# PSUM as two single banks and two groups of three, with the order of head steps around it

## The chip, the cores and the metric

The kernel runs on one core of a Trainium2 chip. The metric is the device time of one execution in microseconds (us). A few per mille separate its runs. Engines are named as in the profile: PE is the matrix engine (TensorE), DVE the vector engine, ACT the scalar engine with activations, POOL is GpSimd, SP the engine that issues most transfers. Each runs its own instructions strictly in the order in which the kernel wrote them, and waits for other engines on semaphores. Matmuls write to PSUM, eight banks of 512 float32 values on each of 128 partitions; ACT and DVE read it from there.

## The reference

Eight images of 8 channels and 256 x 256 pixels go through two layers, all in float32. `_gn` is a group normalization (4 groups of channels).

```python
def _L0_conv_ref(x, ...):           # x: normalized image, G=4 groups, WID=10, 12 x 12 modes
    h = _gconv1x1(concat(x, gridx, gridy), fc0_w, fc0_b)
    for i in range(4):
        h1 = _spectral_conv(h, sp_w1[i], sp_w2[i])   # rfft2, 12 x 12 modes mixed, irfft2
        h2 = _gconv1x1(h, w_w[i], w_b[i])
        h = h1 + h2
        if i < 3:
            h = _gswish(h, betas[i])
    h = _gswish(_gconv1x1(h, fc1_w, fc1_b), betas[3])    # 10 -> 128 channels a group
    return _gconv1x1(h, fc2_w, fc2_b)                    # 128 -> 2 channels a group

x = x + _L0_conv_ref(_gn(x), ...)
x = x + _L1_conv_ref(_gn(x))         # dilation: the maximum of each 3 x 3 window
return x
```

The part around the loop is called the *head* below: fc1, swish, fc2, the sum with x and the statistics of the result. The second layer is the *dilation*.

## The kernel before, in words

**State.** The hidden state of one image lies in `h`, 11 chunks c (`NCH`) of 128 partitions x 4 x 512 values. Three lines of the image share a partition group of 30 rows (`NBLK` x `WID`), so there are 4 partition groups of 32.

**PSUM.** One helper gives out all of it: `ps_z` (L56), four buffers of two banks each, in rotation. `ps_a` (L59) takes such a buffer and uses its first bank. An operation over four groups q takes a pair of buffers: groups 0 and 1 in the first, 2 and 3 in the second. Whoever wants a buffer waits until the buffer's last user but three has been read.

**A layer** (layers 0 to 2 of an image, `layer`, L448) goes over the chunks:

- `burst(c)` (L494): 16 + 8 products into a pair of buffers p_z (the 1x1 convolution, L504 or L501, and the way back from the spectrum, L507), then two ACT operations of 1024 values that write h[c] (swish, L513).
- `turn(c)` (L451): two DVE transpositions of h[c] into `turned`, a ring of three chunks.
- `transform(k)` (L462): the column transform of chunks 2k and 2k+1, 32 products into a pair p_d, copied back into `turned` by DVE (first buffer) and ACT (second), L476.
- `gather(k)` (L478): p_u, 4 products that sum partitions, copied by DVE into the spectrum's input `zt`.

After the last chunk `spectrum_h` (L342) turns `zt` four times on DVE and makes the row transform p_b (L357) on PE; `mix` (L377) does the spectral weights on DVE, 12 operations of 800 values, and folds the result with p_f (L403); `rows_of` (L422) expands the rows, p_g, two of ten channels at a time, ten copies into `zt`.

**Layer 3** only has bursts (without swish, L515, and a store of the chunk to DRAM, `stored`). Between them stands the start of the *next* image, `start` (L560): its statistics and spectrum (`spectrum_x`, L246) and its first mixing. It is a generator called `side` in `layer`, and each `next(side)` records one piece of it: for instance four BN statistics on DVE; or their aggregate on DVE, p_st on PE and what DVE makes of it.

**The head** of the image before is cut into 128 steps (`head`, L631). `first(n)` (L645) reads a stored chunk from DRAM, makes fc1 for the four groups (p_fc1, L651, four products of 512 columns, two passes each) into a pair of buffers, and two ACT operations of 1024 values (swish, L653) into `act`. `second(n)` (L656) makes fc2 of two steps into one bank (L673), which DVE adds to y (L676, L678); every 16 steps y is finished, gets its statistics (L684) and goes to DRAM. In the loop (L691) step n first does `second(n - 4)` when n is even, then `first(n)`.

**The dilation** of the image before that (`dilate`, L702) is a generator, too: per two rows of each partition one load (POOL's queue), about eight DVE operations in several pieces, and a store.

**Who sets the order.** No scheduler: PE, DVE and ACT get their instructions as `fno_dilate_kernel` records them. The main loop (L768) runs over the yields of the layers, and decides at each whether to record a head step: a tuple such as `(1,)` is that many steps, each with one piece of the dilation (`tail`) after it; a number is a share of a step, times `scale`, added up until a whole step is due; "odd" or "even" records one more step if the number of the next one hasn't that parity. In image 0 there is no head to record (`scale` is None), and its layers stand alone. After image 7 the whole last head, 128 steps, stands alone. The head of an image gets all its 128 steps during the next image.

So a round of a layer (L539) is: burst, gather, step (fc2, fc1), dilation piece, turn, burst, transform, step (fc1), dilation piece, turn. A chunk of layer 3 (L532) is: burst, piece of the next image, step (fc1), dilation piece, piece of the next image, step (fc2, fc1), dilation piece.

Of the kernel before, what the change touches and what calls it, by code (L numbers as in the profile page):

```python
# [10 lines left out]
F32 = mybir.dt.float32  # L11
# [8 lines left out]
HW = 256  # L20
NPIX = HW * HW
G = 4
WID = 10
# [21 lines left out]
def fno_dilate_kernel(ctx: ExitStack, tc: tile.TileContext, a: dict, out: bass.AP):  # L45
# [9 lines left out]

    def ps_z(name):  # L56
        return ps.tile([128, 2, 512], F32, tag="z", bufs=4, name=name)

    def ps_a(name):  # L59
        return ps_z(name)[:, 0, :]  # L60

    def part(i):
        return slice(32 * i, 32 * i + 32)
# [89 lines left out]
    wc = const.tile([128, 32], F32, tag="wc", name="wc")  # L153
    p = ps_z("p_wc")
    for g in range(G):
# [37 lines left out]
    def copy(i, dst, src):  # L193
        if alone[0] and i % 2:
            nc.scalar.activation(dst, src, AF.Identity)  # L195
        else:
            nc.vector.tensor_copy(dst, src)  # L197

    def copy_2(i, dst, src):
        if i % 2:  # L200
            nc.scalar.activation(dst, src, AF.Identity)  # L201
        else:
            nc.vector.tensor_copy(dst, src)  # L203


# [40 lines left out]
    def spectrum_x(b, out_):  # L246
# [55 lines left out]
        a3 = a3.rearrange("p (j k) -> p j k", j=2)  # L302
        pair = [ps_z(f"p_xs_{b}_{i}") for i in range(2)]
        for k in range(2):
            for term in range(2):
                for q in range(4):
                    for g in range(G):
                        mm(pair[g // 2][part(q), g % 2, 6 * k : 6 * k + 6], unf[part(g), spectrum_table(k, term), :],
                           a3[part(g), :, 12 * term + 3 * q : 12 * term + 3 * q + 3],
                           start=term == 0, stop=term == 1)  # L310
        xe4 = xe.rearrange("p (s k) g j -> p s g j k", s=2)
        for k in range(2):
            for i in range(2):
                nc.vector.tensor_copy(
                    xe4[:, k, 2 * i : 2 * i + 2, 0:2, :],
                    pair[i][:, :, 6 * k : 6 * k + 6].rearrange("p g (j k) -> p g j k", j=2),
                )
        yield 1.4
# [13 lines left out]
    def spectrum_table(k, term):  # L332

        return 0 if k == term else (1 if k == 0 else 2)
# [87 lines left out]
    def rows_of(b, l):  # L422

        zv = zt[:, :, :, : NBLK * WID].rearrange("p r f (n o) -> p o n r f", n=NBLK)
        for o in range(0, WID, 2):
            p = ps_z(f"p_g_{b}_{l}_{o}")
            for u in range(2):
                if l % 2 == 0:
                    mm(p[:, u, : NBLK * CS * NQ], fz[:, o + u].rearrange("p g k -> p (g k)"),
                       rowg.rearrange("p n j r -> p (n j r)"), start=True, stop=True)  # L430
                else:
                    for g in range(G):
                        for j in range(NQ):
                            mm(p[part(j), u, NBLK * CS * g : NBLK * CS * (g + 1)], fz[:, o + u, g, :],  # L434
                               rowg[:, :, j, :], start=True, stop=True)
            for u in range(2):
                src = p[:, u, : NBLK * CS * NQ]
                if l % 2 == 0:
                    dst = zv[:, o + u].rearrange("p n r f -> p n f r")
                    src = src.rearrange("p (n f r) -> p n f r", n=NBLK, r=CS)  # L440
                else:
                    dst = zv[:, o + u].rearrange("p n r f -> p f n r")
                    src = src.rearrange("p (f n r) -> p f n r", f=NQ, n=NBLK)
                copy(u, dst, src)
            yield 0.7


    def layer(b, l, out_, stored, side):  # L448
        group_in_f = l % 2 == 1

        def turn(c):  # L451

            dst = turned[:, c % 3].rearrange("p (s f x) -> p f s x", s=2, f=NQ)
            for i in range(2):
                nc.vector.transpose(  # L455
                    dst[:, 2 * i : 2 * i + 2], h[:, c, 2 * i : 2 * i + 2].rearrange("p f (s x) -> p f s x", s=2))
# [5 lines left out]
        def transform(k):  # L462


            cs = chunks_of(k)
            n, lo = len(cs), cs[0] % 3
            step = cs[-1] % 3 - lo if n == 2 else 1
            t = turned[:, lo : lo + step * (n - 1) + 1 : step].rearrange("p n (r v i) -> p n r v i", r=2 * NQ, v=8)
            pair = [ps_z(f"p_d_{b}_{l}_{k}_{i}") for i in range(2)]
            for v in range(8):  # L470
                for q in range(NQ):
                    mm(pair[q // 2][part(v % 4), q % 2, : 240 * n], fw8[part(q), v, :],  # L472
                       t[part(q), :, :, v, : NBLK * WID], start=v < 4, stop=v >= 4)
            e = turned[:, (2 * k + 1) % 3, : 960 * n].rearrange("p (q x) -> p q x", q=NQ)
            for i in range(2):
                copy_2(i, e[:, 2 * i : 2 * i + 2], pair[i][:, :, : 240 * n])  # L476

# [16 lines left out]
        def burst(c):  # L494
            pair = [ps_z(f"p_z_{b}_{l}_{c}_{i}") for i in range(2)]
            for f in range(NQ):
                for q in range(NQ):
                    o = pair[q // 2][part(f), q % 2, :]
                    if l == 0:
                        k = slice(32 * q, 32 * q + 6)  # L500
                        mm(o, wcn[k, :], h[k, c, f, :], start=True, stop=False)  # L501
                    else:
                        g = f if group_in_f else q
                        mm(o, wt[part(q), l, g, :], h[part(q), c, f, :], start=True, stop=False)  # L504
            for s in range(2):
                for q in range(NQ):
                    mm(pair[q // 2][:, q % 2, HW * s : HW * (s + 1)],  # L507
                       zt[part(q), 2 * c + s].rearrange("p f o -> p (f o)"), binv[part(q), :],
                       start=False, stop=s == 1)
            for i in range(2):  # L510
                dst = h[:, c, 2 * i : 2 * i + 2, :]
                if l < 3:
                    nc.scalar.activation(dst, pair[i], AF.Silu)  # L513
                else:
                    nc.scalar.activation(dst, pair[i], AF.Identity, bias=bias3)  # L515
            if l == 3:
                nc.sync.dma_start(stored[c], h[:, c].rearrange("p f w -> p (f w)"))
# [11 lines left out]
        if l == 3:  # L529

            yield "odd"
            for c in range(NCH):  # L532
                burst(c)
                for _ in range(LAST):
                    next(side, None)
                    yield (1,)
            return
        yield "even"
        for k in range((NCH + 1) // 2):  # L539
            c = 2 * k  # L540
            burst(c)
            if k > 1:
                gather(k - 2)
            yield (1,)
            turn(c)
            if c + 1 < NCH:
                burst(c + 1)
            if k > 0:
                transform(k - 1)
            yield (1,)  # L550
            if c + 1 < NCH:
                turn(c + 1)
        out_["sw"] = [load_sw(l + 1, 0), load_sw(l + 1, 1)]
# [77 lines left out]
    def head(b, stored, stats):  # L631
# [13 lines left out]
        def first(n):  # L645

            k, blk = n // 32 * NCH + n % 32 // NBLK, n % 32 % NBLK
            act = sb.tile([128, G, 512], F32, tag="act", bufs=4, name=f"act_{b}_{n}")
            pair = [ps_z(f"p_fc1_{b}_{n}_{i}") for i in range(2)]
            for g in range(G):  # L650
                mm(pair[g // 2][:, g % 2, :], w1[part(g), blk, :], hs[k][part(g), :], start=True, stop=True)  # L651
            for i in range(2):
                nc.scalar.activation(act[:, 2 * i : 2 * i + 2, :], pair[i], AF.Silu)  # L653
            acts[n] = act
# [36 lines left out]
        for n in range(STEPS):  # L691
            if n % 32 % NBLK == 0:
                load_state(n // 32 * NCH + n % 32 // NBLK + 2)
            if n % 2 == 0 and n > 3:
                second(n - 4)
            first(n)
            yield
        second(STEPS - 4)
        second(STEPS - 2)
# [61 lines left out]
    with tc.manual_schedule(engines={PE, DVE, ACT}):  # L761
# [3 lines left out]
        for b in range(n_img):  # L765
            stored = [dram.tile([128, NQ * PIX], F32, tag=f"hs{c}", name=f"stored_{b}_{c}") for c in range(NCH)]
            exact, loose, ahead = 0, 0, {}
            for n in layers(b, stored, d, start(b + 1, ahead)):  # L768
                if isinstance(n, str):
                    if count[0] % 2 != (n == "odd") and step():  # L770
                        share -= 1.0
                elif isinstance(n, tuple):
                    exact += sum(n)
                    for _ in range(sum(n)):
                        if scale and step():
                            tail()
                else:
                    loose += n
                    share += n * scale if scale else 0
                    while share >= 1.0:  # L780
                        share -= 1.0
                        step()
# [176 lines left out]
```

## Time and profile before

| | us |
|---|---|
| median of 3 runs | 3963.68 |
| lowest, highest run | 3955.75, 3963.84 |
| the profiled execution | 3959.03 |
| its span, first to last instruction | 3957.2 |
| matmul busy, DVE busy, ACT busy | 3714.1, 2516.6, 2803.0 |
| mean granted PE clock | 0.978 |
| image 0, layers 0, 1, 2 (no head steps) | 52.5, 52.9, 52.8 |
| image 2, layer 0, from first burst to p_b | 88.0 |
| image 2, layer 0 to 1: from p_b to p_f, and to the next burst | 20.4, 19.5 |
| image 2, layer 1, from first burst to p_b | 83.9 |
| image 2, layer 3, up to the first burst of image 3 | 97.2 |
| last head alone, with the last dilation | 282.3 |

The stages are cut at the start of their first PE instruction. One image takes some 470 us, and the first 370 us (loading, image 0) are slower per piece of work. A busy engine in this profile isn't one that computes all the time: an instruction's time holds what it waits for inside the engine, and matmul ends are modelled. Starts are better than busy times: the distance from the start of one group of matmuls to the start of the next (its pitch) can be compared with the same pair elsewhere.

In the lines below, a row in order of time reads: start, duration, engine, source line, operation, tile written <- tiles read, shape, count; in brackets how long the engine had been idle and what released it. A row of a group ends with busy time, mean duration in ns, idle time before and its releasers. A row of a stretch has its time, then the busy time of PE, weight loads, DVE, ACT and POOL with instruction counts, then the granted PE clock (1.00 is full), the share of DMA and GB/s.

### The profile page before, as it was taken

Reading aid. Unit: us, or ns where it says so; the run is one execution under the profiler, and the core shown is the slowest. Engines: PE = TensorE matmul, PEld = TensorE weight load, DVE = VectorE, ACT = ScalarE, POOL = GpSimd, SP = SyncE. Lnnn points to the kernel's source line nnn. Section 1 sums busy time; section 2 is a strip of 40 time slices with the busy share of each in tenths; the row PEclk is TensorE's granted clock in tenths of the full one; section 3 lists DMA queues with packets and bytes.
Section 4 is the critical chain, followed back from the end, with each engine's and each line's share of the span. In section 5 each row is a group of like instructions: output and inputs, shape, how many; then the busy total and the mean of one; then the engine's idle time right before and its main releaser. Section 6 shows DMA issues by size and latency. Waiting matters only on the chain. (4 is left out here: it accounts for less than half of the span.)

```text
span 3957.2 us, 119367 instructions
## 1 busy us (share of the span) xinstructions
PE 3714.1 (94%) x53882; PEld 1423.3 (36%) x53882; DVE 2516.6 (64%) x3740; ACT 2803.0 (71%) x2933; POOL 117.4 (3%) x202
## 2 busy tenths in 40 slices
PE   5667999999999999999999999999999999999996
PEld 2334333333333333333333333333333333333221
DVE  6775656556766666766766576766676666673533
ACT  3335777777777777776777777777777777778886
POOL 1000000000000000000000000000000000000000
PEclk8878999999999999999999999999999999999998
DMA  3014111432225222251223511244221532215311
GB/s 87 14 44 165 55 35 45 145 115 66 61 62 180 87 60 62 86 195 50 60 59 100 195 52 50 62 135 146 60 61 50 175 107 60 60 53 198 103 46 45
DMA packets 114132, 345.08 MB, mean 87 GB/s; under 512 B 16040, under 2 KB 18536, under 8 KB 98200
## 3 DMA queue, kind: packets, MB, share of 16 engines
q1 hardware_dynamic: 95432, 276.32, 22.4%
q0 software_dynamic: 18192, 61.13, 4.7%
q8 instruction: 424, 6.95, 0.7%
q14 instruction: 84, 0.69, 0.1%
HBM read 213.39 MB, written 123.74 MB: 85 GB/s over the span
## 5 line engine op out<-in xcount | busy, mean ns | idle before, releaser
L653 ACT ACTIVATE act<-p_fc 128x1024 f32<-128x1024 f32 x2048 | 1961.1, 1026 | 718.9 <-PE p_fc L651 718.0
L651 PE MATMUL p_fc<-hs,c_w 32*128 32x512 f32 x8192 | 1191.2, 631 | 2.4 <-DVE h L676 1.1
L673 PE MATMUL p_fc<-act,c_w 128*32 128x512 f32 x8192 | 986.7, 600 | 49.8 <-ACT act L653 37.0
L651 PEld LDWEIGHTS p_fc<-hs,c_w 32*128 32x128 f32 x8192 | 389.6, 183 | 683.2 <-ACT act L653 294.9
L455 DVE STREAM_TRANSPOSE turned<-h 128x1024 f32<-128x1024 f32 x528 | 622.6, 1218 | 13.4 <-ACT h L513 13.3
L513 ACT ACTIVATE h<-p_z 128x1024 f32<-128x1024 f32 x528 | 511.9, 1021 | 122.4 <-PE p_z L507 121.8
L678 DVE TENSOR_TENSOR y<-p_fc,y 128x512 f32<-128x512 f32 x392 | 270.6, 690 | 462.4 <-PE p_fc L673 462.4
L673 PEld LDWEIGHTS p_fc<-act,c_w 128*32 128x32 f32 x8192 | 226.5, 109 | 673.0 <-issue 413.3
L507 PE MATMUL p_z<-c_binv,zt 32*128 32x256 f32 x5632 | 409.3, 404 | 1.0 <-ACT zt L195 1.0
L507 PEld LDWEIGHTS p_z<-c_binv,zt 32*128 32x128 f32 x5632 | 258.5, 186 | 307.0 <-issue 288.6
L504 PE MATMUL p_z<-h,c_wt 32*32 32x512 f32 x8448 | 358.5, 603 | 5.6 <-DVE y L678 2.7
L472 PE MATMUL p_d<-turned,c_fw 32*32 32x480 f32 (+1 forms) x9216 | 304.9, 541 | 1.4 <-DVE turned L455 1.4
L197 DVE COPY zt<-p_g 128x264 f32<-128x264 f32 x300 | 161.0, 628 | 178.4 <-PE p_g L434 91.8
L203 DVE COPY turned<-p_d 128x960 f32<-128x960 f32 x144 | 154.3, 1072 | 159.4 <-PE p_d L472 158.9
L515 ACT ACTIVATE h<-p_z,c_bias 128x1024 f32<-128x1024 f32 x176 | 186.6, 1111 | 57.9 <-PE p_z L507 57.6
L387 DVE TENSOR_REDUCE S<-turned 128x80 f32<-128x800 f32 x192 | 188.9, 984 | 5.2
L384 DVE TENSOR_TENSOR turned<-t,B 128x800 f32<-128x800 f32 x192 | 188.5, 982 | 0.2
L348 DVE STREAM_TRANSPOSE turned<-zt 128x960 f32<-128x960 f32 x96 | 175.0, 1849 | 0.8
L201 ACT ACTIVATE turned<-p_d 128x960 f32<-128x960 f32 x144 | 130.3, 905 | 59.4 <-PE p_d L472 59.4
L472 PEld LDWEIGHTS p_d<-turned,c_fw 32*32 32x32 f32 x9216 | 121.3, 103 | 141.3 <-issue 79.0
L504 PEld LDWEIGHTS p_z<-h,c_wt 32*32 32x32 f32 x8448 | 84.8, 103 | 226.4 <-issue 60.3
L486 PE MATMUL p_u<-turned,c_stack 128*32 128x480 f32 (+1 forms) x1152 | 136.2, 544 | 15.6 <-DVE turned L203 15.6
(177 smaller groups left out, 1846.9 us busy)
## 6 DMA issues: line engine op xcount, KB each, us to landing
stored<-h SPq DMA_DIRECT2D x88, 1024.0 KB
hs<-stored SPq DMA_DIRECT2D x352, 256.0 KB
t<-in_spw SPq DMA_DIRECT2D x96, 400.0 KB
yin<-y_rows POOLq DMA_DIRECT2D x56, 512.0 KB, 4.8
h<-in_xp SPq DMA_DIRECT2D x352, 48.0 KB
turned<-in_xw SPq DMA_DIRECT2D x16, 1024.0 KB
y<-in_x SPq DMA_DIRECT2D x56, 256.0 KB
y_rows<-y POOLq DMA_DIRECT2D x56, 256.0 KB, 2.6
```

The costliest lines, as they stand in the source:

```text
L384: nc.vector.tensor_tensor(pr, sw[k], bt[:, k2, k].unsqueeze(2).to_broadcast([128, G, 2 * WID, WID]), ALU.mult)
L387: nc.vector.tensor_reduce(s[k2][:, k].rearrange("p g s o -> p (g s o)"), pr.rearrange("p g m i -> p (g m) i"), AX.X, ALU.add,)
L455: nc.vector.transpose(dst[:, 2 * i : 2 * i + 2], h[:, c, 2 * i : 2 * i + 2].rearrange("p f (s x) -> p f s x", s=2))
L472: mm(pair[q // 2][part(v % 4), q % 2, : 240 * n], fw8[part(q), v, :], t[part(q), :, :, v, : NBLK * WID], start=v < 4, stop=v >= 4)
L504: mm(o, wt[part(q), l, g, :], h[part(q), c, f, :], start=True, stop=False)
L507: mm(pair[q // 2][:, q % 2, HW * s : HW * (s + 1)], zt[part(q), 2 * c + s].rearrange("p f o -> p (f o)"), binv[part(q), :], start=False, s ...
L513: nc.scalar.activation(dst, pair[i], AF.Silu)
L515: nc.scalar.activation(dst, pair[i], AF.Identity, bias=bias3)
L651: mm(pair[g // 2][:, g % 2, :], w1[part(g), blk, :], hs[k][part(g), :], start=True, stop=True)
L653: nc.scalar.activation(act[:, 2 * i : 2 * i + 2, :], pair[i], AF.Silu)
L673: mm(acc[part(g), :], w2[:, g, 15 - rb - i : 47 - rb - i], act[:, g, :], start=i == 0, stop=i == 1)
L678: nc.vector.tensor_tensor(y, sums, y, ALU.add)
```

## The change

PSUM is given out in two kinds: `one`, a single bank, two buffers; and `tri`, three banks, two buffers. What took a pair of two-bank buffers now takes one of each (`ps_four`): group 0 in the single bank, groups 1 to 3 in the three. ACT's two operations on such a result are of 512 and 1536 values rather than 1024 each. In the column transform DVE copies group 0 (480 values) and ACT groups 1 to 3 (1440). Row expansion goes three, three and four channels at a time, and asks for five whole steps at fixed places, from an odd one on.

In the head, `second` now follows `first`: step n does `first(n)`, and, if n is odd, `second(n - 3)`. In layers the turning of a chunk is split into halves and set around the transform or the step, the transform stands ahead of the second burst, and the dilation's pieces are recorded where a layer yields "tail", behind a turning. In layer 3 each chunk is: burst, step (fc1, fc2), dilation piece, piece of the next image, step (fc1), dilation piece, piece of the next image.

```diff
-    def ps_z(name):
-        return ps.tile([128, 2, 512], F32, tag="z", bufs=4, name=name)
-
     def ps_a(name):
-        return ps_z(name)[:, 0, :]
+        return ps.tile([128, 512], F32, tag="one", bufs=2, name=name)
+
+    def ps_tri(name):
+        return ps.tile([128, 3, 512], F32, tag="tri", bufs=2, name=name)
+
+    def ps_four(name):
+        one, tri = ps_a(f"{name}_0"), ps_tri(f"{name}_1")
+        return one, tri, [one] + [tri[:, i, :] for i in range(3)]
...
     def rows_of(b, l):
-        for o in range(0, WID, 2):
-            p = ps_z(f"p_g_{b}_{l}_{o}")
-            for u in range(2):
+        yield "odd"
+        for os_ in (range(0, 3), range(3, 6), range(6, 10)):
+            name = f"p_g_{b}_{l}_{os_[0]}"
+            if len(os_) == 4:
+                banks = ps_four(name)[2]
+            else:
+                tri = ps_tri(name)
+                banks = [tri[:, i, :] for i in range(3)]
+            for u, o in enumerate(os_):
...
-            yield 0.7
+            yield (1, 1) if len(os_) == 3 else (1,)
...
-        def turn(c):
+        def turn(c, halves=(0, 1)):
...
-            for i in range(2):
+            for i in halves:
...
         def transform(k):
...
-            for i in range(2):
-                copy_2(i, e[:, 2 * i : 2 * i + 2], pair[i][:, :, : 240 * n])
+            nc.vector.tensor_copy(e[:, 0], one[:, : 240 * n])
+            nc.scalar.activation(e[:, 1:4], tri[:, :, : 240 * n], AF.Identity)
...
         def burst(c):
...
-            for i in range(2):
-                dst = h[:, c, 2 * i : 2 * i + 2, :]
+            for dst, src in ((h[:, c, 0, :], one), (h[:, c, 1:4, :], tri)):
                 if l < 3:
-                    nc.scalar.activation(dst, pair[i], AF.Silu)
+                    nc.scalar.activation(dst, src, AF.Silu)
...
         if l == 3:
             yield "odd"
             for c in range(NCH):
                 burst(c)
                 for _ in range(LAST):
+                    yield (1,)
+                    yield "tail"
                     next(side, None)
-                    yield (1,)
             return
         yield "even"
         for k in range((NCH + 1) // 2):
...
             if k > 1:
                 gather(k - 2)
             yield (1,)
-            turn(c)
+            turn(c, (0,))
+            if k > 0:
+                transform(k - 1)
+            turn(c, (1,))
+            yield "tail"
             if c + 1 < NCH:
                 burst(c + 1)
-            if k > 0:
-                transform(k - 1)
-            yield (1,)
-            if c + 1 < NCH:
-                turn(c + 1)
+                turn(c + 1, (0,))
+                yield (1,)
+                turn(c + 1, (1,))
+                yield "tail"
+            else:
+                yield (1,)
...
         def first(n):
...
-            for i in range(2):
-                nc.scalar.activation(act[:, 2 * i : 2 * i + 2, :], pair[i], AF.Silu)
+            nc.scalar.activation(act[:, 0, :], one, AF.Silu)
+            nc.scalar.activation(act[:, 1:4, :], tri, AF.Silu)
...
         for n in range(STEPS):
...
-            if n % 2 == 0 and n > 3:
-                second(n - 4)
             first(n)
+            if n % 2 and n > 2:
+                second(n - 3)
             yield
-        second(STEPS - 4)
         second(STEPS - 2)
...
             for n in layers(b, stored, d, start(b + 1, ahead)):
-                if isinstance(n, str):
+                if n == "tail":
+                    if scale:
+                        tail()
+                elif isinstance(n, str):
...
                     for _ in range(sum(n)):
-                        if scale and step():
-                            tail()
+                        if scale:
+                            step()
```

## The prediction

> **What bounds the kernel now.** I read the page's first part, then the groups by shape, then stretches in order of time.
>
> ```profile
> PE 3714.1 (94%) x53882; PEld 1423.3 (36%) x53882; DVE 2516.6 (64%) x3740; ACT 2803.0 (71%) x2933; POOL 117.4 (3%) x202
> ```
>
> PE sets the pace: 3957.2 us of span, 243 without a matmul, most of that in image 0. But starts inside a group can also be spread by a wait, so I took pitches, start of a group to start of the next. Undisturbed, one head step's fc1 (8 passes) takes 0.96 to 1.07 us, the fc2 of two steps 1.85, a burst 2.08, a column transform 2.17, p_u 0.83.
>
> ```profile
> L653 ACT ACTIVATE act<-p_fc 128x1024 f32<-128x1024 f32 x2048 | 1961.1, 1026 | 718.9 <-PE p_fc L651 718.0
> L201 ACT ACTIVATE turned<-p_d 128x960 f32<-128x960 f32 x120 | 116.6, 972 | 33.0 <-PE p_d L472 33.0
> L201 ACT ACTIVATE turned<-p_d 128x480 f32<-128x480 f32 x24 | 13.7, 571 | 26.4 <-PE p_d L472 26.4
> L455 DVE STREAM_TRANSPOSE turned<-h 128x1024 f32<-128x1024 f32 x528 | 622.6, 1218 | 13.4 <-ACT h L513 13.3
> ```
>
> ACT's price is (972 - 571) / 480 = 0.835 ns an element and 0.17 us fixed. Now head steps alone, near the end (PE, then ACT):
>
> ```profile
> 3806.31 1.92 PE L673 MATMUL p_fc<-act,c_w 128*32 128x512 f32 x16
> 3808.17 2.01 PE L651 MATMUL p_fc<-hs,c_w 32*128 32x512 f32 x16
> 3810.48 1.92 PE L673 MATMUL p_fc<-act,c_w 128*32 128x512 f32 x16 [0.30 <-ACT act L653]
> ...
> 3809.40 3.77 ACT L653 ACTIVATE act<-p_fc 128x1024 f32<-128x1024 f32 x4 [1.26 <-PE p_fc L651]
> 3813.57 1.02 ACT L653 ACTIVATE act<-p_fc 128x1024 f32<-128x1024 f32 x1 [0.39 <-PE p_fc L651]
> ```
>
> A pair of steps repeats every 4.17 us (3809.40 to 3813.57), though PE needs 3.72 (0.96 + 0.91 + 1.85) and ACT 3.77. fc2 waits until ACT's first 1.02 us operation frees a pair of banks, 3809.40 + 1.03 + 0.05 = 3810.48; fc2 and the next fc1 then leave ACT idle for 0.39. Layers 0 to 2 have nearly none of this: one round (two bursts, a transform, a p_u, two steps) takes 11.56 us, and the same pitches add up to 11.4.
>
> In layer 3 the next image's start is threaded in:
>
> ```profile
> 1699.37 1.20 PE L651 MATMUL p_fc<-hs,c_w 32*128 32x512 f32 x8
> 1699.51 0.69 DVE L678 TENSOR_TENSOR y<-p_fc,y 128x512 f32<-128x512 f32 x1 [0.41 <-PE p_fc L673]
> 1700.12 2.46 DVE L256 BATCH_NORM_STATS2 bn_x<-turned 128x6 f32<-128x512 f32 x4
> 1702.50 0.41 DVE L260 BATCH_NORM_AGGREGATE mv_x<-bn_x 128x2 f32<-128x12 f32 x4
> 1702.54 1.19 PE L651 MATMUL p_fc<-hs,c_w 32*128 32x512 f32 x8
> 1703.91 0.39 PE L241 MATMUL p_st_x<-mv_x,avg 128*128 128x4 f32 x2 [0.19 <-ACT h L515]
> ```
>
> fc2 ends at 1699.37; the sum, four statistics and their aggregate end 3.5 us later, while PE does fc1, a burst and fc1 (4.5 us). p_st finds its input ready.
>
> **The change, part by part.** Sums are in us against this execution.
>
> *Banks of one and three, steps alone.* ACT keeps two operations a step: 0.60 and 1.45 us, together the 2.05 of 2 x 1.026. No row shows 1536 elements; 1.45 goes by the slope, 1.54 by one and a half of the 1024 row; I take 1.45, three rows lying on that line. fc2 now needs the single bank only, free 0.65 after ACT starts, before PE reaches it. What then closes the loop is the second three-bank group: its operation ends 3.76 after ACT's start, PE does fc1, fc2, fc1 (0.05 + 0.96 + 1.85, then 1.2 from start of fc1 to ACT), 7.82 us for two periods, so 3.91 a pair. The last 64 pairs gain 0.25 each: **-16** (0 if the wait only moves, -25 at ACT's 3.77).
>
> *Steps between mixings and row expansions* (21 layers: 1 to 3 of images 1 to 7). Before, three such waits of 0.43 and one of 0.6 a mixing; after, 0.19 each, and 0.5 once, where four mixing operations (0.92 each) and a sum (0.61) outlast 3.91: 0.95 saved. Row expansion with fixed steps saves another 0.35 at its first product: **-27** (0 to -40). No operation is added to rows; the ten copies of 0.63 stay on DVE behind 15 us of PE work.
>
> *Layer ends.* Before, p_u waits 0.63 for DVE's copy, the next fc2 some 0.7 for ACT, two pairs 0.43 each: 2.2. After, an fc1 and an fc2 lie between transform and p_u, but the last two zt turnings (1.83 each) come behind a late sum and hold p_b about 1.25: -0.96 in 21 layers, **-20** (-40 to +10).
>
> *Layer starts and rounds.* A three-bank group is held 0.11 + 0.49 + 1.45 + 0.05 = 2.1 us after a burst. The second burst follows with only an fc1 between (1.1 stall), transform 0 likewise (1.05), later transforms with p_u and fc1 between (0.2 each, four times): 2.95. Gone are 0.87 at the third burst and six times 0.15, the dearer burst after fc1. 1.1 to 1.2 x 21: **+23** (0 to +35). The uneven split (DVE 1.16 to 0.66, ACT 0.97 to 1.37 a transform) costs nothing: a round has 8.5 us of DVE and 9.6 of ACT in 11.56; uncovered it would cost 0.4 x 126 = 50. Halved turnings ahead of the sum delay it by one turning (1.2); the bank it frees is wanted 2 us later.
>
> *Layer 3, without threaded work.* fc2 waits 0.2 to 0.34 for ACT's first 1.1 us operation; 0.69 is enough afterwards. 77 chunks x 0.15: **-11** (-25 to +5).
>
> *Layer 3, threaded work.* fc2 now comes before the threaded pieces, so every DVE operation of both pieces and both dilation calls is queued behind the sum, which waits for fc2, and a PE operation that needs them has one fc1 (1.0) before it, not fc1, burst, fc1. In the changed order of images 3 to 6, p_st follows fc2, fc1, and on DVE sum, two o maxima, four statistics, the closing of o, the aggregate: 0.14 + 0.61 + 1.2 + 2.46 + 1.53 + 0.5 = 6.4, a stall of 5.4. p_a1: 0.14 + 0.61 + 0.6 + 1.15 + 1.53 + 0.1 = 4.1, 3.0 too late. a3: 1.1, p_f: 1.2. Queued behind each are the burst or fc1, then ACT's activations and the store of h. 10.7 in four images, 9.5 in image 2 (fewer dilation operations), 5 in image 1 (none): **+57** (0 if DVE is early after all, +70).
>
> *Image 0* has no steps, so nothing is between a turning and its transform but a burst and p_u:
>
> ```profile
> 171.45 2.19 PE L472 MATMUL p_d<-turned,c_fw 32*32 32x480 f32 x61
> ...
> 174.80 2.36 DVE L455 STREAM_TRANSPOSE turned<-h 128x1024 f32<-128x1024 f32 x2
> ...
> 179.08 1.39 PE L472 MATMUL p_d<-turned,c_fw 32*32 32x480 f32 x33
> ```
>
> Now 7.63 a round. With the transform ahead of the second burst it must wait for that chunk of the round before: ACT 2.04, turning 2.5, 4.6 after its burst, against 3.0 of PE work: 8.85 a round, five rounds, three layers: **+20** (0 to +27).
>
> *Clock.* Stretches of half clock occur without any idle as long as these:
>
> ```profile
> 3212.00:3226.00 14.00, 14.00 (x159) 4.77 (x139) 6.58 (x20) 6.32 (x7) 0.00 (x0) 0.64 0.02 7
> ```
>
> Here 0.64 over 14 us, five of them lost. I take one stretch of some 5 us at half clock, 2.5 lost, for each of the six images with new gaps: **+15** (0 to +40, two longer ones each). [...]
>
> *Transfers.* Their number is unchanged. On SP's queue the threaded pieces' loads (x, spectral weights) now stand behind that step's hs and y loads instead of ahead; x is read three pieces, some 9 us, after its issue, and DVE's waits show none for it today; a late one would hold the statistics by what it is late. On POOL's queue the dilation's loads and stores move by under one step, and DVE waited 20 us for them in the whole execution. Both are costed at nothing.
>
> **Sum.** -16 - 27 - 20 + 23 - 11 + 57 + 20 + 15 = +41: span 3998, run 3959.0 + 41 = 4000. The median shown, 3963.7, lies 4.7 above the profiled run, so about 4005.
>
> **Rivals.** *A, the threaded work stays covered* (faster): if DVE runs ahead so that p_st and p_a1 do not wait, both last terms vanish, 41 - 57 - 15 = -31, 3933. For it: today these pieces cost PE under 0.5 each, and DVE is 64% busy. Against: the sum waits for fc2 in the queue ahead of them. It decides below some 25 us of such stalls in all (41 - 15 - 57 + 1.26 times the stalls, the clock scaled with them), 4 an image. *B, the waits are dearer* (slower): groups of three and clock at their upper ends, 41 + 12 + 13 + 25 = +91, 4055. For it: half clock already comes in layer 0 with 0.5 us gaps. Against: full clock in other layers. *C, no effect beyond the measurement*: stalls half as long, 41 - 28 - 8 = +5, 3969; gains and losses cancel, and the fewer waits are paid back in layer 3.
>
> **How the numbers follow.** Forecast 0.62, A 0.17, B 0.12, C 0.09. The time is the forecast's, 4005, its own range 3975 to 4035. The range goes to 3945 (most of A left out) and 4050 (most of B). 0.2%, 8 us, is what a measurement here can tell from no change. Faster 0.18 (A and a rest), same 0.09, slower 0.73.
>
> **What would show it.** Right: in layer 3, p_st with an idle of 4 to 6 us before it released by DVE's aggregate, p_a1 2 to 4; pairs at the end every 3.9 us; transforms of image 0 8.8 apart; second bursts waiting 1 us for ACT. Wrong: no idle before p_st, or 1536 elements well over 1.5 us, or pairs still 4.17 apart.

## The result, and the profile after

The changed kernel takes 4058.0 us (median of 4 runs, 4050.7 to 4063.4), the one before 3959.9 us: a ratio of 1.0247, 95% interval 1.0225 to 1.0268. It is slower by 98 us, where +41 was forecast; the time lies above the range. The profiled execution has a span of 4055.8 us (before 3957.2: +98.6) and a mean granted clock of 0.970 (before 0.978).

The page's first part, of the changed kernel:

```profile
PE 3687.1 (91%) x53882; PEld 1433.9 (35%) x53882; DVE 2457.6 (61%) x3744; ACT 2836.7 (70%) x2929; POOL 117.0 (3%) x202
```

The same matmuls; PE's busy time fell by 27 us while the span rose by 99. What grew is time without a matmul. The waits of PE name where (source line, tile and what it waited for; us in total, times, longest):

```profile
PE p_f L399 <- DVE F L391: 75.3, 25, 12.9
PE p_st_x L238 <- DVE mv_x L257: 45.4, 7, 17.8
PE p_b L353 <- DVE turned L344: 29.7, 23, 7.5
...
PE p_fc L658 <- ACT act L659: 14.3, 32, 1.2
...
PE p_z L504 <- DVE wcn L530: 8.1, 7, 1.4
```

Before, p_f waited for F 42.8 us in 4 places (image 0 and its start), p_st_x for mv_x 3.9 in one, p_b 14.9 in 2, and no wait for wcn stands in the list. Of p_st's 45.4 us the longest wait, 17.8, is no loss of the change: it is the start of the program, where this p_st came at 16.43 us before and comes at 17.79 now. The other six are in layer 3. Here wcn is the convolution weights of layer 0, scaled on DVE with the image's statistics (L530).

The groups by shape (busy, mean ns of one, idle before) give the prices that had to be guessed:

```profile
L660 ACT ACTIVATE act<-p_fc 128x1536 f32<-128x1536 f32 x1024 | 1492.2, 1457 | 0.0
...
L680 PE MATMUL p_fc<-act,c_w 128*32 128x512 f32 x8192 | 987.6, 600 | 5.4 <-ACT act L659 5.4
...
L659 ACT ACTIVATE act<-p_fc 128x512 f32<-128x512 f32 x1024 | 614.8, 600 | 455.9 <-PE p_fc L658 442.6
...
L479 ACT ACTIVATE turned<-p_d 128x1440 f32<-128x1440 f32 x120 | 164.5, 1371 | 86.1 <-PE p_d L475 86.1
```

1.457 and 0.600 us for 1536 and 512 elements: the slope's 1.45 and 0.60 hold. fc2 waits 5.4 us for ACT in the whole execution, 50 before. So what the change was costed to remove is removed. Head steps alone, near the end (start, duration):

```profile
3989.86 1.92 PE L680 MATMUL p_fc<-act,c_w 128*32 128x512 f32 x16
...
3993.67 1.92 PE L680 MATMUL p_fc<-act,c_w 128*32 128x512 f32 x16
...
3997.76 1.92 PE L680 MATMUL p_fc<-act,c_w 128*32 128x512 f32 x16
```

A pair takes 3.81 and 4.09 us here, in the median of the last 62 pairs 3.96 (before 4.17, forecast 3.91).

**Layer 3.** p_st in image 3, in order of time, all engines:

```profile
1765.08 1.14 PE L658 MATMUL p_fc<-hs,c_w 32*128 32x512 f32 x8
1765.18 0.69 DVE L685 TENSOR_TENSOR y<-p_fc,y 128x512 f32<-128x512 f32 x1 [0.77 <-PE p_fc L680]
1765.79 0.68 DVE L731 TENSOR_TENSOR o<-m 128x512 f32<-128x512 f32 x1
...
1766.50 0.69 DVE L732 TENSOR_TENSOR o<-o,m 128x512 f32<-128x512 f32 x1
...
1767.11 2.46 DVE L253 BATCH_NORM_STATS2 bn_x<-turned 128x6 f32<-128x512 f32 x4
1769.49 0.53 DVE L735 TENSOR_SCALAR o<-o,mr_y 128x512 f32<-128x512 f32 x1
...
1770.94 0.42 DVE L257 BATCH_NORM_AGGREGATE mv_x<-bn_x 128x2 f32<-128x12 f32 x4
...
1771.51 0.56 PE L238 MATMUL p_st_x<-mv_x,avg 128*128 128x4 f32 x2 [5.29 <-DVE mv_x L257]
...
1772.21 2.03 PE L507 MATMUL p_z<-h,c_wt 32*32 32x512 f32 x32
...
1774.17 2.09 PE L510 MATMUL p_z<-c_binv,zt 32*128 32x256 f32 x16
```

The queue on DVE is the forecast one, sum, two maxima, four statistics, the closing of o, aggregate, and PE idles 5.29 us (forecast 5.4). Then the next burst takes 3.8 us instead of 2.1, at half clock (granted clock 0.50).

**Image 0.** Its column transforms (p_d), PE's operations in order of time:

```profile
169.18 3.63 PE L475 MATMUL p_d<-turned,c_fw 32*32 32x480 f32 x64 [2.38 <-DVE turned L458]
...
179.57 2.17 PE L475 MATMUL p_d<-turned,c_fw 32*32 32x480 f32 x60 [1.37 <-DVE turned L458]
...
188.44 2.12 PE L475 MATMUL p_d<-turned,c_fw 32*32 32x480 f32 x57 [1.37 <-DVE turned L458]
```

8.87 us from the second to the third (forecast 8.85), 7.63 before; the 10.4 ahead of it has a transform largely at half clock (granted clock 0.55 over its 3.63 us).

**Where the 98.6 us lie.** I cut the span into stages at the first matmul of each kind, as in the table of before, and for images 1 to 7 took off 1.00 us for each fc1 and 1.85 for each fc2 of two steps, since the change moves steps between stages; so the differences are estimates. The start of image 0 ends at image 1's first p_g, layer 3 of a later image at the next image's first p_f. The last column is the us that half clock took (time x (1 - granted clock)), which the measured column holds already.

| stage | before | changed | difference | forecast | clock, before to changed |
|---|---|---|---|---|---|
| image 0, layers 0 to 2 | 158.5 | 186.8 | +28 | +20 | 6.8 to 14.9 |
| start, rest of image 0 | 205.2 | 208.2 | +3 | 0 | 51.8 to 55.1 |
| images 1 to 7, layers 0 to 2 | 998.3 | 967.3 | -31 | +3 (-20 + 23) | 11.9 to 6.8 |
| images 1 to 7, row transform, mixing, row expansion up to the first burst | 308.4 | 369.2 | +61 | -27 | 2.8 to 6.8 |
| layer 3, images 1 to 6 | 230.5 | 279.6 | +49 | +46 (-11 + 57) | 1.7 to 23.9 |
| image 7's layer 3, last head | 85.4 | 73.5 | -12 | -16 | 12.3 to 14.9 |

The clock, forecast at +15 for all stages, makes +35. Without the steps taken off, layer 3 of images 1 to 6 went from 461.5 to 527.7. Its +49 looks like the +46 that was forecast, but 22 of it is half clock, which the forecast counted apart; without it layer 3 grew by 27. The +61 is also of more than the forecast's 21 stretches behind p_b: some 43 of it lie in these, and some 18 in the seven row expansions ahead of layer 0, for which the sum has no term.

### The profile page after: what moved, and what is told of

The parts are those of the page before. It is cut to its first block, busy times and chain, and to the rows that moved or that the text cites. A ratio compares the mean times of both kernels' runs of the same rounds, so it can differ in the third digit from the quotient of the medians.

```text
span 4055.8 us, 118770 instructions
## 1 busy us (share of the span) xinstructions
PE 3687.1 (91%) x53882; PEld 1433.9 (35%) x53882; DVE 2457.6 (61%) x3744; ACT 2836.7 (70%) x2929; POOL 117.0 (3%) x202
## 4 chain that ended last, share of the span: by engine, by line
PE 72%; DVE 16%; ACT 5%; issue 5%; DMA 1%; POOL 0%; DVEq 0%; POOLq 0%; ACTq 0%; SPq 0%
PE p_fc L658 19%; PE p_fc L680 18%; PE p_z L510 8%; PE p_d L475 7%; PE p_z L507 6%; ACT h L515 4%; DVE turned L458 2%; PE p_b L353 2%; DVE turned L344 2%; PE p_z L504 2%; PE p_g L437 2%; PE p_g L432 2%; DVE y L685 2%; PE p_u L489 2%; DVE S L383 2%
## 5 line engine op out<-in xcount | busy, mean ns | idle before, releaser
L660 ACT ACTIVATE act<-p_fc 128x1536 f32<-128x1536 f32 x1024 | 1492.2, 1457 | 0.0
L658 PE MATMUL p_fc<-hs,c_w 32*128 32x512 f32 x8192 | 1175.1, 632 | 37.5 <-ACT act L659 14.3
L659 ACT ACTIVATE act<-p_fc 128x512 f32<-128x512 f32 x1024 | 614.8, 600 | 455.9 <-PE p_fc L658 442.6
L458 DVE STREAM_TRANSPOSE turned<-h 128x1024 f32<-128x1024 f32 x528 | 648.5, 1234 | 317.9 <-ACT h L515 317.4
L515 ACT ACTIVATE h<-p_z 128x512 f32<-128x512 f32 (+1 forms) x528 | 511.8, 1021 | 279.5 <-PE p_z L510 279.5
L507 PE MATMUL p_z<-h,c_wt 32*32 32x512 f32 x8448 | 376.4, 617 | 15.6 <-DVE y L685 10.2
L475 PE MATMUL p_d<-turned,c_fw 32*32 32x480 f32 (+1 forms) x9216 | 329.6, 545 | 36.2 <-DVE turned L458 21.7
L517 ACT ACTIVATE h<-p_z,c_bias 128x512 f32<-128x512 f32 (+1 forms) x176 | 186.6, 1110 | 141.8 <-PE p_z L510 141.6
L479 ACT ACTIVATE turned<-p_d 128x1440 f32<-128x1440 f32 x144 | 183.0, 1271 | 137.2 <-PE p_d L475 137.2
L478 DVE COPY turned<-p_d 128x480 f32<-128x480 f32 x144 | 88.7, 616 | 139.2 <-PE p_d L475 138.0
```

Source lines behind the costliest of these rows:

```text
L458: nc.vector.transpose(dst[:, 2 * i : 2 * i + 2], h[:, c, 2 * i : 2 * i + 2].rearrange("p f (s x) -> p f s x", s=2))
L475: mm(banks[q][part(v % 4), : 240 * n], fw8[part(q), v, :], t[part(q), :, :, v, : NBLK * WID], start=v < 4, stop=v >= 4)
L515: nc.scalar.activation(dst, src, AF.Silu)
L658: mm(banks[g], w1[part(g), blk, :], hs[k][part(g), :], start=True, stop=True)
L659: nc.scalar.activation(act[:, 0, :], one, AF.Silu)
L660: nc.scalar.activation(act[:, 1:4, :], tri, AF.Silu)
```

## The experiments

Unless said otherwise an edit is made on the changed kernel (4058), three rounds, each beside runs of the kernel before. "Ratio" is to the kernel before.

**Layer 3 in its old order** (fc2 ahead of fc1 in these steps too, by lines of `head` that are not shown here):

```diff
             for c in range(NCH):
                 burst(c)
                 for _ in range(LAST):
+                    next(side, None)
                     yield (1,)
                     yield "tail"
-                    next(side, None)
```

> The changed kernel (4058), with the order of layer 3 alone put back: piece of the next image, step, dilation piece, and fc2 ahead of fc1 in these steps. Theory (the threaded pieces wait on DVE behind the sum and the dilation, and the gap before p_st drops the clock): 45 to 65 us come back, 3993 to 4013; p_st's wait falls from 45 us in seven to under 10, and the half-clock time of images 1 to 7 from some 80 us to some 35. Rival 1 (it is the bank groups that slow layer 3): 4045 to 4060. Rival 2 (half clock comes from elsewhere): the wait goes, half clock stays, 4015 to 4030.

Measured: 4004.8, ratio 1.0108 (1.0088 to 1.0129). 53 us come back, as the theory had it. p_st's wait is 25.7 us in six (17 of them in image 0's start), layer 3 of images 1 to 6 takes 455.4, less than before, and half clock there takes 8.5 us instead of 23.9. So of the 53 some 15 are clock. Two parts of the expectation came only in part: half clock in images 1 to 7 ahead of the last head fell from 75 us to 49, not to 35, and p_st still waits where the dilation's piece now stands behind the step:

```profile
1752.64 0.36 PE L238 MATMUL p_st_x<-mv_x,avg 128*128 128x4 f32 x2 [1.68 <-DVE mv_x L257]
```

**Image 0's transform in its old place**, behind the second burst:

```diff
-            if k > 0:
+            if k > 0 and b > 0:
                 transform(k - 1)
...
                 burst(c + 1)
+            if k > 0 and b == 0:
+                transform(k - 1)
```

> The changed kernel, with the transform of image 0 alone put back behind the second burst. Theory: its three layers went from 52.8 to 62.3 us by that place alone, so they return to within 2 us of 52.8: 28 us less, 4030 (4024 to 4036). Rival (the three-bank groups, which only leave two bursts in flight, cost it): layers stay above 58 us, 4045 to 4058.

Measured: 4030.8, ratio 1.0165 (1.0149 to 1.0180), 27 us less. Layers 1 and 2 take 53.1 us, as before; layer 0 58.0, of which half clock takes 8.9 (before 2.1). So the place of the transform costs 22 of the 28 us. The other 5.4, in layer 0, stay as in the rival's case, and they came with the bank groups: with the groups alone (below) layer 0 takes the same 58.0, with the same 8.9 of half clock.

**Three fixed steps in the row expansion**, one behind each product, instead of two, two and one:

```diff
-            yield (1, 1) if len(os_) == 3 else (1,)
+            yield (1,)
```

The reason, in the changed kernel's row expansion of image 3, layer 1 (in order of time):

```profile
1482.90 1.59 PE L437 MATMUL p_g<-c_rowg,fz 128*32 128x66 f32 x96
...
1483.48 1.45 ACT L660 ACTIVATE act<-p_fc 128x1536 f32<-128x1536 f32 x1
1484.42 1.70 PE L658 MATMUL p_fc<-hs,c_w 32*128 32x512 f32 x8
...
1484.98 0.31 PEld L658 LDWEIGHTS p_fc<-hs,c_w 32*128 32x128 f32 x6 [0.27 <-ACT act L660]
...
1486.04 1.92 PE L680 MATMUL p_fc<-act,c_w 128*32 128x512 f32 x16
```

p_g's product holds one of the two groups of three, the fc1 ahead of it the other, which ACT reads until 1484.93. The fc1 behind p_g starts its first product at 1484.42, in the single bank, and goes on with the three only then: fc2 follows after 1.62 us instead of 1.07.

> The changed kernel with one step instead of two behind each three-channel product of the row expansion (three fixed steps instead of five; the other two fall into the shares between the mixings). Theory: with fc1, p_g, fc1 in a row the second fc1 asks for the three-bank group that ACT still reads, 0.55 us twice a row expansion, 28 row expansions; with fc2 always between, these 31 us go: 4027 (4015 to 4040). Rival (the steps meet the same wait between mixings, or the loss there is DVE's): 4050 to 4070.

Measured: 4032.2, ratio 1.0178 (1.0161 to 1.0195), 26 us less. With the steps taken off, row expansions fall by 20 us (194.5 to 174.4) and the other stages of the layers by 11; for these 11 no cause is shown. So in the rows the group of three is what costs, but the trace corrects the count: the first of the two waits stays, and the second goes because an fc2 now stands ahead of that p_g.

**The bank groups alone**, on the kernel before, with its orders and shares of steps:

```diff
-    def ps_z(name):
-        return ps.tile([128, 2, 512], F32, tag="z", bufs=4, name=name)
+        return ps.tile([128, 512], F32, tag="one", bufs=2, name=name)
+    def ps_tri(name):
+        return ps.tile([128, 3, 512], F32, tag="tri", bufs=2, name=name)
...
-        for o in range(0, WID, 2):
+        for os_ in (range(0, 3), range(3, 6), range(6, 10)):
...
-            yield 0.7
+            yield 0.35 * len(os_)
```

> The kernel before with the bank groups alone (one and three, with the copies and activations that follow from it); every order and share of steps as before. Theory (the order costs the time, the groups are about neutral: last head -12 to -16, second bursts +1.1 a layer): 3945 to 3990, image 0 within 3 us a layer of before, p_st without a wait over 2 us. Rival (groups of three are what costs): 4020 or more.

Measured: 3986.1, ratio 1.0059 (1.0044 to 1.0074): 23 us dearer than before, inside the range. The last head gains 8, the layers 3; layer 3 and layer 0 of image 0 lose some 6 each, and with them half clock grew (12 and 7 us); mixings and row expansions lose 30, where p_g now waits for a group of three:

```profile
PE p_g L436 <- ACT act L654: 16.6, 14, 1.2
...
PE p_g L431 <- ACT act L654: 8.3, 7, 1.2
```

**The orders alone**, with the PSUM of before in the changed kernel (buffers of two banks again, rows two channels at a time):

```diff
     def ps_a(name):
-        return ps.tile([128, 512], F32, tag="one", bufs=2, name=name)
+        return ps_z(name)[:, 0, :]
...
-        for os_ in (range(0, 3), range(3, 6), range(6, 10)):
+        for o in range(0, WID, 2):
...
-            yield (1, 1) if len(os_) == 3 else (1,)
+            yield (1,)
```

> The changed kernel with the PSUM of before (four buffers of two banks; rows two channels at a time with one fixed step each): all new orders, old groups. Theory (orders and groups cost separately; groups alone were +23): 4058 - 23 = 4035 (4015 to 4050), p_st's wait as in the changed kernel. Rival (the orders are only dear with groups of three): under 4000.

Measured: 4122.3, ratio 1.0400 (1.0385 to 1.0416). Both fell: the parts don't add up. The orders alone cost 155 us (4122.3 - 3967.3), and given them the groups are worth 64. The reason stands in fc2's idle time:

```profile
L679 PE MATMUL p_fc<-act,c_w 128*32 128x512 f32 x8192 | 990.0, 601 | 83.6 <-ACT act L659 38.0 <-ACT h L514 26.0 <-ACT h L516 16.8
```

fc2 right behind fc1 asks for a buffer of two banks that ACT is still reading, 84 us in all; with a single bank of its own it waits 5.4. So the new head order needs the new groups, and the groups without it are a loss.

**The three edits together**, layer 3, image 0 and rows:

> The changed kernel with the three edits together: layer 3 in its old order, image 0's transform behind the second burst, three fixed steps in the row expansion. Theory (three separate losses): their single gains add up, 53 + 27 + 26 = 106, 3952 (3940 to 3965). Rival (the losses share the half-clock time or the same waits, so that one edit takes part of another's gain): 3970 to 4000.

Measured: 3947.9, ratio 0.9957 (0.9944 to 0.9970), faster than before. 110 us come back, against 106 for the sum: to within the noise the three losses are separate.

**p_st one piece later**, in the new layer 3:

```diff
             nc.vector.bn_aggr(mv[:, g], st[:, g].rearrange("p n s -> p (n s)"))
+        yield 2.8
         p = ps_a(f"p_st_x{b}")
```

> The changed kernel, its layer 3 in the new order, with one cut more in the start of the next image: p_st is recorded one piece after the aggregate that it reads. Theory (p_st waits because the aggregate stands right before it, behind the sum and the dilation on DVE; the clock falls after that gap): p_st's wait falls from 45 us in seven to under 22 (16.5 of them in image 0's own start), 25 us of waiting go, and half of the half-clock time of layer 3 (8 us lost): 4025 (4015 to 4035). Rival (the gap is not what drops the clock): 4030 to 4038, with layer 3's clock loss still above 20 us.

Measured: 4042.9, ratio 1.0203 (1.0183 to 1.0224): only 15 us, a miss. The wait went as expected (17.2 us in four, all but 0.5 in one wait of image 0's start) and layer 3 fell by 36 us to 491.9, half clock in it from 23.9 to 10.2. But half clock took 20.5 us more in layer 0, behind a gap that the changed kernel has, too, and 17.0 more in row expansions and 14.6 more between p_f and p_g, in good part behind gaps that this edit made longer. In the start of the next image, the changed kernel and then the one with the edit (image 3):

```profile
1835.03 1.02 PE L399 MATMUL p_f<-F,c_fold 32*32 32x120 f32 x32 [1.09 <-DVE F L391]
```

```profile
1824.80 1.02 PE L400 MATMUL p_f<-F,c_fold 32*32 32x120 f32 x32 [2.07 <-DVE F L392]
...
1828.64 2.98 PE L433 MATMUL p_g<-c_rowg,fz 128*128 128x264 f32 x6 [2.66 <-DVE fz L201]
```

This p_f waits 2.0 to 2.3 us in six images (1.1 in the changed kernel), and p_g 2.66 in five (1.62); behind these two the changed kernel has one window of half clock in all (3.4 us, image 5), and here 6.8 or 10.2 us at half clock follow in each of the six. So a part of the wait was not taken away but moved on along the next image's start. (The profiled execution is the slowest of the four, 4054.5; its parts overstate this loss against the median.)

**p_st one piece later, and wcn ahead of the row expansion:**

```diff
+        if l == 0:
+            out_["wcn"] = sb.tile([128, 32], F32, tag="wcn", bufs=1, name=f"wcn_{b}")
+            nc.vector.tensor_scalar(out_["wcn"], wc, out_["mr"][:, 1:2], None, ALU.mult)
         yield "odd"
```

> The kernel whose p_st is recorded one piece after its aggregate (4043, 27 us lost to half clock in layer 0 of images 1 to 7), with wcn made ahead of the row expansion. Theory (the 1.1 us gap in which layer 0's first burst waits for wcn starts the half clock that follows it): the 8 us of waiting go and with them 15 to 20 us of half clock, 4018 (4008 to 4028), layer 0's clock loss under 12 us. Rival (the half clock there comes from the six-row products of layer 0 themselves): 8 us only, 4035, with over 20 us of clock loss left in layer 0.

Measured: 4029.4, ratio 1.0149 (1.0131 to 1.0166). Layer 0's loss to the clock fell from 27.3 to 8.5 us and the wait for wcn is gone. The 15 us around the start of layer 0 of image 5, without and with the edit (the granted clock is the third figure from the end):

```profile
2336.00:2351.00 15.00, 13.52 (x134) 5.12 (x130) 5.37 (x7) 7.54 (x8) 0.00 (x0) 0.66 0.07 19
```

```profile
2323.50:2338.50 15.00, 14.31 (x198) 5.40 (x190) 6.88 (x10) 8.67 (x9) 0.00 (x0) 0.89 0.11 31
```

So most of that half clock needed the gap of 1.1 us in front of the first burst. The gap alone does not make it: the changed kernel has the same seven waits for wcn, 8.1 us in both, and loses 6.8 us to the clock in layer 0. The whole gain stayed 1 us short of its bounds, since layer 3 lost 8.6 us more to the clock than without the edit.

**The three edits and the early wcn**:

> The kernel with the three edits together, and layer 0's scaled weights wcn made by DVE before the row expansion instead of behind its last sum. Theory: the first burst of layer 0 waits 8.0 us in seven for wcn, which go: 7 us below the kernel with the three edits, 3945 (3933 to 3958). Rival (the burst then waits for the last rows' copies instead): no difference over 3 us.

Measured: 3939.2, ratio 0.9939 (0.9920 to 0.9958), 9 us below the three edits, as expected to within 2, though the runs of the two overlap (up to 3947.6 here, from 3945.8 there).

**A step in front of p_f**, on that kernel and on the changed kernel:

```diff
         nc.vector.tensor_tensor(f[:, 1], s[0][:, :, :, 1, :], s[1][:, :, :, 0, :], ALU.add)
-        yield 0.5
+        yield "odd"
+        yield (1,)
```

> The kernel with the three edits and the early wcn (3939), and one step that has an fc2 (fc1, fc2) recorded between the last two operations of the mixing on DVE and p_f. Theory (p_f waits because the last reduction stands on DVE behind the sum of a late fc2, with one fc1 of PE work left): the 24 us of p_f's wait outside image 0 go, and the half clock that follows these gaps (5 us): 3915 (3905 to 3930). Rival (the step is then missing between p_f and p_g, which waits for p_f's copies instead): 3930 to 3945, with 15 us or more of new waits at p_g.

> The changed kernel with that one edit alone: a step with an fc2 between the mixing's last two operations and p_f. Theory: p_f's wait falls from 75 us in 25 to about 43 in four (image 0's), and the half clock between p_f and p_g (5 us) goes: 4025 (4015 to 4038). Rival (waits move to p_g): 4040 to 4060.

Measured: 3932.9, ratio 0.9931 (0.9917 to 0.9945), and 4051.4, ratio 1.0230 (1.0209 to 1.0250): 6 and 7 us below, less than runs of one of these kernels differ by, and the rival's case both times. The waits of PE in the faster kernel show where p_f's wait outside image 0 went (64.2 us in 17 places before the edit, so 19):

```profile
PE p_f L400 <- DVE F L391: 45.5, 4, 13.0
PE p_b L353 <- DVE turned L344: 42.5, 17, 7.5
...
PE p_g L436 <- DVE fz L201: 11.3, 6, 1.9
...
PE p_g L441 <- DVE fz L201: 8.6, 6, 1.4
```

p_f now waits in image 0 alone, but p_g waits 20 us for the copies of p_f, for which no such wait for DVE is listed before the edit, and p_b 7 us more. A step given to one wait is missing at the next. That is what one expects where the chain on DVE (p_b, mixing, p_f, copies) sets the length of the stretch; from p_b to p_g it still fell by 12 us in 21 layers, steps taken off, so the chain is not all of it. The profiled run on the changed kernel lost 24 us more to half clock besides.

**The transform behind the second burst in all images**, on the kernel with the three edits and the early wcn:

```diff
-            if k > 0 and b > 0:
-                transform(k - 1)
...
-            if k > 0 and b == 0:
+            if k > 0:
                 transform(k - 1)
```

> The kernel with the three edits and the early wcn (3939), its transforms behind the second burst in all images, not in image 0 alone. Theory (with groups of three only two bursts or transforms can be in flight, so the second burst, one fc1 behind the first, waits 1.1 us each round for ACT; a transform between them covers that): 5 rounds x 21 layers x 0.3 to 0.5 us dearer, 3980 (3965 to 3995). Rival (the place of the transform is neutral where there are steps): 3932 to 3947.

Measured: 3964.4, ratio 1.0004 (0.9994 to 1.0015), 25 us dearer, just under the theory's range. Layers 0 to 2 take 23 us more. The second burst behind fc1 now waits in every round, two products, then over a microsecond until ACT has read the group:

```profile
2055.69 1.04 PE L664 MATMUL p_fc<-hs,c_w 32*128 32x512 f32 x8
2056.66 1.04 PE L510 MATMUL p_z<-h,c_wt 32*32 32x512 f32 x2
2057.88 1.15 PE L510 MATMUL p_z<-h,c_wt 32*32 32x512 f32 x30 [0.18 <-ACT h L518]
```

With steps in the round the new place of the transform is a gain (25 us here); in image 0, without them, it is a loss (27 us).

## Why the prediction was wrong

**Its sign and the mechanism of its largest term held. One term had the wrong sign, and missed by more than the whole forecast did; the layers, better than forecast, hide a part of that.**

- *Steps between mixings and row expansions, -27*: the step that failed; the stage measured +61, 88 off in a miss of 57. The sentence "No operation is added to rows" counted operations and not groups of PSUM: in the fixed order fc1, p_g, fc1 the second fc1 waits for a group of three that ACT is reading. Three fixed steps instead of five gave back 31 us in the profile of images 1 to 7 (20 in the row expansions). The sum took the one long wait of a mixing as 0.5 us; outside image 0 p_f waited up to 2.08. And nothing stood in it for wcn ahead of layer 0 (8.7 us in the median, by the early wcn). With these and the step before p_f the stage is at 315.8 us, 7 above before: the gain that was forecast for it never appeared. That a faster pair of steps can't shorten a stretch whose chain runs over DVE is the likely reason, argued from the waits that moved from p_f to p_g and p_b, not shown alone. By its own terms the saving was too high as well: (3 x 0.43 + 0.6) - (3 x 0.19 + 0.5) is 0.82, not 0.95.
- *Layer ends and rounds, -20 + 23*: measured -31. The forecast saw nothing to gain in a round, 11.56 us against pitches said to add up to 11.4; these pitches add up to 10.9 to 11.2. From one transform to the next, in the middle rounds of layers 1 and 2 of images 2 to 7, the changed kernel takes 11.2 us, with the transform behind the second burst 11.5, with the groups alone 11.8. So the wait for a group of three behind a burst was costed, but not that the transform between the bursts covers it; its old place costs 23.
- *Layer 3, threaded work, +57*: right in mechanism, and for image 3 in size. There p_st waits 5.3 (forecast 5.4), p_a1 takes 4.95 us to the next group instead of 1.74, 3.2 more (3.0), a3 waits 0.9 (1.1), p_f 1.1 (1.2): 10.5 against 10.7. Over all six images it is less: putting the order back takes 40 us from layer 3 without the clock (55 with it), and leaves p_st 8.7 of waiting. That DVE's work stands behind the sum was shown twice, by the order and by the later p_st.
- *Layer 3 without threaded work, -11*: in its old order layer 3 is 6 us below before in spite of 7 us more half clock, so about right. That the stage's +49 meets the +46 of both terms is luck: without half clock it is +27.
- *Clock, +15*: mis-sized, +35; 22 in layer 3, 8 in image 0's layers. One stretch of 5 us an image was assumed; they were one to four stretches of 3.4 or 6.8.
- *Image 0, +20*: the pitch was right (8.87 against 8.85), the measured +28 holds 8 us of clock, of which 5 came with the groups and not with the place.
- *Steps alone, -16*: -12.
- *Rival B* (dearer waits and clock, 4055) hit the number, mostly for another reason: its 25 for the clock is near the 20 that came, but it put 12 on the groups in the layers and 13 on the threaded work, and neither lost more than forecast. *Rival A* fell with the 5.29 us at p_st.

What stays open is why half clock moves between stages when one gap is closed. The edits that put back a place or a count came within 1 to 5 us of what was expected (layer 3, image 0, rows). Those that pushed work on along a chain missed by 18 to 26 (the later p_st, the step before p_f): a wait came back further on, and on the changed kernel half clock with it.

## What to carry to other kernels

Here the larger PSUM group was the scarcer one (with the bank groups alone p_g waited 16.6 + 8.3 us for ACT's reads, 2.1 + 2.1 before): before giving three banks to an operation, list everything that asks for such a group between two of its uses, small products too, and not only the operation that gets faster. When work is threaded into another engine's order, place what waits (here a sum behind fc2, with 5.29 us of idle PE in front of image 3's p_st) after the work that others need, or let a piece lie between producer and consumer. Two parts of one change need not add up (here +23 and +155 alone, +98 together, and -19 to -29 once the places that lost were put back): test them apart and together.

## What the runs showed of the hardware

In each of the 14 profiles all stretches at half clock start within 4 ns of a grid of 3.413 us and last a multiple of it (but for the last one, which outlasts the program). "Window" below is one step of this grid. In the changed kernel half clock also followed a window in which PE worked. Three windows around a p_f (time, PE busy, ..., granted clock):

```profile
2199.98:2203.40 3.42, 3.42 (x35) 0.99 (x32) 3.30 (x4) 2.83 (x5) 0.00 (x0) 1.00 0.73 243
2203.40:2206.81 3.41, 1.48 (x12) 0.31 (x8) 3.04 (x6) 3.37 (x4) 0.00 (x0) 1.00 0.31 94
2206.81:2210.22 3.41, 3.27 (x40) 1.94 (x40) 1.65 (x5) 0.02 (x1) 0.00 (x0) 0.50 0.23 90
```

The window with PE busy for 1.48 of 3.41 us was granted 1.00, the next one 0.50. Counted over the 14 profiles, from 392 us on and up to PE's last instruction, over windows that were at full clock themselves and without those in or just behind a layer 0 (first burst to p_b): after windows in which PE was busy for under 45%, 109 of 111 were at half clock; after 45 to 60%, 37 of 157; after 60% or more, 26 of 11661. In the profiles of the kernel before and of the changed kernel together these are 11 of 11, 1 of 14 and 4 of 1682. An estimate from these counts: a gap of 2 us that falls into one window leaves 41% of it busy, in the first class; cut in two it leaves some 71% of each window, in the last. By this estimate an edit that shifts everything by a microsecond can change which gaps are followed by half clock, which fits the moves seen above, though no run shifted the work alone to prove it. In layer 0, whose products with wcn use 6 rows (6*32, 6x512 in the trace), half clock came after 23 of 1942 windows that were busy for over 90%, elsewhere after 7 of 10585; why is not shown.
